# Layer 0's product in moving blocks of 512 only, multiplied and summed by VectorE, with the mean taken out beforehand

## The chip, the cores and the metric

The kernel runs on one core of a Trainium2 chip. The core has five engines with queues of their own: TensorE (PE in the profile; its weight loads are listed as PEld), VectorE (DVE), ScalarE (ACT), GpSimd (POOL) and SyncE (SP, which here only issues DMAs). Matmuls write to PSUM, from which VectorE and ScalarE read. The metric is the device time of one execution in microseconds; lower is better. Three runs of the kernel before took 760.51, 760.79 and 761.57 us.

## What is computed

A graph of N = 2048 nodes has B = 8 batches of C = 64 features. Two layers follow each other, each with a residual and a layer norm (subtract the mean over the 64 features, divide by the root of the variance):

```
w = einsum('nd,dkio->nkio', embedding, weight)     # D = 16, K = 3: a weight matrix of its own for every node
b = einsum('nd,do->no', embedding, bias)
A_stack = [I, A, 2 A A - I]
out = einsum('bnki,nkio->bno', einsum('knm,bmc->bnkc', A_stack, x), w) + b
x = layernorm(x + out)                              # layer 0
x = layernorm(x + [x, Ax, 2AAx - x, Ax, 2AAx - x] @ W1 + b1)   # layer 1
```

For layer 0 the kernel never builds `w`. For a tile of 128 nodes it computes, for each batch and each of the 16 embedding dimensions d, the product of the node features (three hops, 64 inputs each) with `weight[d]` (64 outputs), and then adds the 16 results up, each scaled with the node's own `embedding[n, d]`.

## The kernel before

The 2048 nodes are 16 tiles of 128. `z[0]`, `z[1]`, `z[2]` hold three feature arrays in SBUF, one row of 512 numbers (8 batches of 64) per node. The core goes through these stages; nearly every instruction is kept in the order in which the Python code emits it (`ordered`, `tc.keep_in_program_order`), so each engine's queue has the order of the code.

1. First hop (`hop_x`, line 526; about 7 to 123 us of the span): A times x, in 32 steps, two passes `g` over 16 row tiles.
2. Second hop (`seven_products`, line 603; 123 to 226 us): A times the first hop, split into seven block products of eight steps each. A step is eight matmuls of 512 columns. In `run` (line 266) the loads of a step are emitted four steps ahead, its operands two to four steps ahead. `more` (line 779) hangs extra work on steps: `load_weights` puts the DMAs of layer 0's weights on SP's queue, and `piece` emits one instruction of `weights()` and `weight_parts()`; they are taken from the list `todo`, two per step.
3. The mix (`mix0`, line 404, and `project`, line 475; 226 to 525 us): the product of layer 0 described above, tile after tile, with the layer norm of the tile before beside it, and layer 1's weights applied to it.
4. Two more hops for layer 1 and the final norm (`third`, `hop_g`, `hop_tile`).

The mix is where the change works. All products are made of three terms (`w_parts`: a high, a low and a mixed part of the numbers, so that float32r matmuls give full accuracy), for three hops, and two batches at once: batch 2u in partitions 0 to 63 and 2u+1 in 64 to 127. So one block of output takes 3 x 3 pairs of matmuls with 64 rows each; the two of a pair go to two PSUM banks (`pm[:, j]`). A tile's work is eight *pieces*, each filling one PSUM tile of two banks; four such tiles go round (`psum`, line 74).

- `by_batch` (line 419) makes one batch pair and eight d: 9 pairs of matmuls, 512 columns wide. ScalarE evicts it with eight scaled copies (line 430), one per d. For `g = 0` GpSimd then adds the copies up in a tree (`sum_aside`, line 444), for `g = 1` the copies are written with a stride, and VectorE sums over d with one reduce (`reduce_aside`, line 454).
- `by_four` (line 432) makes two batch pairs and four d: 18 pairs, 256 columns wide. VectorE takes it in with four scalar_tensor_tensor (line 440), each of which scales one d and adds it to the tile's sum `acc`.

A tile has four pieces of each sort, in this order; a pair (g, i) with i below 2 is `by_batch`:

```
pieces, on_vector = [(1, 0), (0, 4), (1, 1), (0, 0), (0, 1), (0, 5), (1, 4), (1, 5)], (1,)
```

The list `at[n]` holds what is emitted before piece n. `begin_sum` (line 391) starts the tile's sum with the features and the bias, in two GpSimd instructions that put the batches into the order of `acc`. `layernorm` (line 360) takes the mean with a VectorE reduce (line 363), subtracts it on GpSimd (line 366), squares on ScalarE, reduces on VectorE (line 371) and scales on GpSimd (lines 377 to 382). Beside that, `operands` (line 743) prepares the next tile: it transposes the first hop on TensorE into a PSUM tile `pt` (line 301), which ScalarE and then VectorE (lines 313 and 315) read. Late in a tile `transpose` (line 304) turns the normed tile before around, into `hT`, and `project` multiplies it with layer 1's weights into two PSUM tiles `pu`.

The last tile has another order of pieces, four that GpSimd sums and none that VectorE reduces, and among them `early` (line 860) emits the first operands of stage 4.

Of the kernel before, what the change touches and what calls it, by code (L numbers as in the profile page):

```python
# [18 lines left out]
P = 128  # L19
# [3 lines left out]
DG = 4  # L23
EPS = 1e-5
# [5 lines left out]
SPLIT = 4096.0  # L30

# [8 lines left out]
def pattern(  # L40
# [127 lines left out]

    def weights():
# [13 lines left out]
        mean = const.tile([P, 4], F32, tag="mean", name="mean")  # L183
# [15 lines left out]
    def weight_parts():  # L199
        vec = nc.vector  # L200
        yield vec.tensor_sub(w[0], w[0], w[2])
        yield vec.tensor_scalar_mul(w[2], w[2], 2.0)
        for k in (0, 2, 1):
            yield nc.scalar.copy(w_high[k], w[k])
            yield vec.tensor_tensor(w_low[k], w[k], w_high[k], ALU.subtract)
            yield vec.scalar_tensor_tensor(w[k], w_low[k], SPLIT, w_high[k], ALU.mult, ALU.add)
            yield vec.tensor_scalar_mul(w_mixed[k], w[k], SPLIT / (SPLIT - 1.0))
            yield vec.tensor_scalar_mul(w_low[k], w_low[k], -SPLIT)
        yield vec.tensor_scalar_mul(emb_sb, emb_sb, 1.0 - 1.0 / SPLIT)

# [149 lines left out]
    def layernorm(src):  # L360

        s = work.tile([P, B], F32, tag="ln_s", name="s")
        ordered(nc.vector.tensor_reduce(s, src, AX.X, ALU.add))
        ordered(nc.vector.tensor_tensor(s, s, part, ALU.mult))
        xc = xcpool.tile([P, B, C], F32, tag="ln_xc", name="xc")
        ordered(nc.gpsimd.tensor_tensor(xc, src, wide(s), ALU.subtract))
        yield xc.rearrange("p b c -> p (b c)")
        sq = squares(xc)
# [13 lines left out]
        ordered(nc.gpsimd.tensor_tensor(xc, xc, wide(r), ALU.mult))  # L382
# [7 lines left out]

    def begin_sum(t):

        acc = work.tile([P, B, C], F32, tag="acc", name="acc")
        for g in range(2):
            ordered(nc.gpsimd.tensor_tensor(
                acc[:, 4 * g : 4 * g + 4, :].rearrange("p (j i) c -> p j i c", j=2),
                bc(0, t)[:, 4 * g : 4 * g + 4, :].rearrange("p (i j) c -> p j i c", j=2),
                ebias[:, t : t + 1, :].unsqueeze(1).to_broadcast([P, 2, 2, C]), ALU.add,
            ))
        return acc  # L400
# [3 lines left out]
    def mix0(t, tt, acc, at, pieces, on_vector=()):  # L404

        def block(pm, lhsT, ds):
            for k in range(3):
                for n in range(3):
                    for j in range(2):
                        q = slice(j * C, (j + 1) * C)  # L410
                        nc.tensor.matmul(  # L411
                            pm[:, j], lhsT=tt[k][n][q, lhsT, :], rhs=w_parts[n][k][q, ds, :],
                            start=(k == 0 and n == 0), stop=(k == 2 and n == 2),
                        )

        def e(d):
            return emb_sb[:, t, d : d + 1]

        def by_batch(g, i):
            pm = bank("pm").rearrange("p j (d c) -> p j d c", c=C)  # L420
            block(pm, 2 * g + i, slice(0, 2 * DG))
            if g in on_vector:
                aside[g, i] = rawp.tile([P, 2, C, 2 * DG], F32, tag="raw", name="aside")
                to = [aside[g, i][:, :, :, d] for d in range(2 * DG)]
            else:
                if i == 0:
                    aside[g] = [rawp.tile([P, DG, 2, 2, C], F32, tag="raw", name="aside") for _ in range(2)]
                to = [aside[g][d // DG][:, d % DG, :, i, :] for d in range(2 * DG)]
            for d in range(2 * DG):
                ordered(nc.scalar.activation(to[d], pm[:, :, d, :], AF.Copy, scale=e(d)))  # L430

        def by_four(g, dg):
            dg -= 2
            pm = bank("pm").rearrange("p j (i d c) -> p j i d c", i=2, d=DG)
            for i in range(2):
                block(pm[:, :, i], 2 * g + i, slice(dg * DG, (dg + 1) * DG))
            for d in range(DG):
                part = acc[:, 4 * g : 4 * g + 4, :]
                got = pm[:, :, :, d, :].rearrange("p j i c -> p (j i) c")
                ordered(nc.vector.scalar_tensor_tensor(part, got, e(dg * DG + d), part, ALU.mult, ALU.add))  # L440

        aside = {}

        def sum_aside(g):
            one, other = [a.rearrange("p d j i c -> p d (j i) c") for a in aside[g]]
# [3 lines left out]
        def add_aside(g):  # L449
            part = acc[:, 4 * g : 4 * g + 4, :]  # L450
            one = aside[g][0][:, 0].rearrange("p j i c -> p (j i) c")
            ordered(nc.gpsimd.tensor_tensor(part, part, one, ALU.add))

        def reduce_aside(i):
            if i == 0:
                aside["sum"] = xcpool.tile([P, 2, 2, C], F32, tag="ln_xc", name="both")
            ordered(nc.vector.tensor_reduce(aside["sum"][:, i], aside[1, i], AX.X, ALU.add))

        def add_reduced(_):
            part = acc[:, 4:8, :].rearrange("p (j i) c -> p i j c", j=2)  # L460
            ordered(nc.vector.tensor_tensor(part, part, aside["sum"], ALU.add))

        does = {"sum": sum_aside, "add": add_aside, "reduce": reduce_aside, "add_reduced": add_reduced}
        for n, (g, i) in enumerate([*pieces, (None, None)]):
            for work_here in at[n]:
                if isinstance(work_here, tuple):
                    for part in work_here[0]:
                        does[part](work_here[1])
                else:
                    work_here()  # L470
            if n < len(pieces):
                (by_batch if i < 2 else by_four)(g, i)
        return layernorm(acc)
# [52 lines left out]
    def hop_x(g, kk, j):  # L526
# [45 lines left out]
        def use(got):  # L572
# [13 lines left out]
            else:  # L586
                ordered(nc.scalar.dma_start(out=corner[kk, :, g, :], in_=seen[:, 0]))
            if last and g == 1:
# [14 lines left out]
    def seven_products(s, to, sums, more, wait=4, raw=(), pairs=((0, 1), (2, 3))):  # L603
# [6 lines left out]
        def sum_of_y(kk, name):  # L610
# [11 lines left out]
            if name == "T2":  # L622
                if kk % 2 == 0:
                    tag = "acc" if kk < KK // 2 else "ln_sq"
                    kept[kk // 2] = work.tile([P, 2, BC], F32, tag=tag, name="t2")
# [109 lines left out]
    accs = []  # L735
# [40 lines left out]
    def piece():  # L776
        ordered(next(pieces))

    more = {
        (0, 3): [  # L780
# [3 lines left out]
        1: [piece] * 11,  # L784
        (2, 0): [lambda: load_weights(0, 2)],
        (3, 0): [lambda: load_weights(1)],
        2: [piece] * 8,
        3: [piece] * 8,
        4: [piece] * 2,
# [5 lines left out]
        (6, 7): [lambda: all_of(first_tile[4]), lambda: first_tile.append(begin_sum(0))],  # L795
    }
    second = seven_products(1, to_z2, sums2, more, raw=((0, 0),))
# [74 lines left out]
    acc, h, norm = first_tile[5], None, None  # L872
    tt = first_tile[0]
    coming = operands(1)
    for t in range(NT):
# [4 lines left out]
        if not last:  # L880
# [3 lines left out]
            at[1] += [n1, lambda: got.update(acc=begin_sum(t + 1))]  # L884
# [3 lines left out]
            at[2] += [n2, go(of_hop), go(of_hop), (("reduce",), 0)]  # L888
            at[3] += [root]
            at[4] += [n3, go(of_second), (("reduce",), 1), (("add_reduced",), 1)]  # L890
            if t + 2 < NT:
                at[4] += [lambda: got.update(coming=operands(t + 2))]
            at[5] += [go(of_second), go(of_second)]
            at[6] += [(("sum",), 0)]
            at[7] += [lambda: got.update(hT=transpose(h, "hT"))] if t else []
            at[7] += [(("add",), 0)]
            pieces, on_vector = [(1, 0), (0, 4), (1, 1), (0, 0), (0, 1), (0, 5), (1, 4), (1, 5)], (1,)
        else:
            at[1] += [n1, n2, root]
            at[2] += [n3, lambda: early(0, "y_high", *s)]  # L900
# [498 lines left out]
```

## Time and profile before

One execution was taken with the profiler: 761.79 us, of which the span from the first to the last instruction is 759.9 us.

| | busy, us | share of the span |
|---|---|---|
| TensorE, matmuls | 750.5 | 99% |
| VectorE | 560.4 | 74% |
| ScalarE | 455.1 | 60% |
| GpSimd | 232.9 | 31% |

The matmuls of line 411 (the pieces of the mix) carry 34% of the chain that ended last, more than any other line. TensorE's granted clock was 0.999 of full speed over the span. In the mix one tile takes 18.74 us. A busy time counts each moment once, a mean does not: the 512 evictions of line 430 have a mean of 484 ns, but with their overlap they take 143.9 us, 281 ns each. Shares over the whole span are of little use here; the views that matter are of one tile of the mix, and of the stages that get new work.

### The profile page before, as it was taken

How to read it: one execution, taken by the hardware profiler on the slowest of the kernel's cores; microseconds unless marked ns; L12 is line 12 of the kernel's file. 1: busy time of each engine (PE TensorE's matmuls, PEld its weight loads, DVE VectorE, ACT ScalarE, POOL GpSimd, SP SyncE). 2: the span in 40 equal slices, each digit the busy share in tenths (PEclk: the TensorE clock that was granted, in tenths of full speed). 3: DMA queues.
4: the chain of work that ended last, by engine and by line, in shares of the span. 5: the costliest groups of instructions: out<-in, count | busy, mean ns of one | idle time of the engine just before them, and what ended most of it. 6: DMA issues, size and time to landing. Idle time of an engine off the chain costs nothing.

```text
span 759.9 us, 15977 instructions
## 1 busy us (share of the span) xinstructions
PE 750.5 (99%) x6094; PEld 666.6 (88%) x6094; DVE 560.4 (74%) x1114; ACT 455.1 (60%) x1106; POOL 232.9 (31%) x267
## 2 busy tenths in 40 slices
PE   9999999999999999999999999999999999999996
PEld 6888888888879999999999999998788888888885
DVE  6768777678748888888888888876688548768663
ACT  5447543878756777777777777767887663112111
POOL 0000000000033666666666666656100000021431
PEclk9999999999999999999999999999999999999999
DMA  9998987555510000000000000003454454565621
GB/s 320 367 391 294 333 282 270 161 174 169 162 58 16 17 19 16 22 19 16 16 16 16 16 16 2 2 16 110 140 168 143 135 170 133 182 180 179 196 97 46
DMA packets 73700, 96.64 MB, mean 127 GB/s; under 512 B 5008, under 2 KB 48528, under 8 KB 73488
## 3 DMA queue, kind: packets, MB, share of 16 engines
q1 hardware_dynamic: 62208, 76.66, 31.9%
q10 hardware_dynamic: 11408, 18.89, 6.8%
q8 instruction: 50, 0.82, 0.5%
q14 instruction: 34, 0.28, 0.1%
HBM read 76.65 MB, written 18.87 MB: 126 GB/s over the span
## 4 chain that ended last, share of the span: by engine, by line
PE 97%; ACT 1%; POOL 1%; DMA 0%; DVE 0%; issue 0%; POOLq 0%; DVEq 0%
PE pm L411 34%; PE accT L682 27%; PE acc L255 15%; PE a L255 10%; PE accT L255 6%; PE pu L483 3%; PE pt L301 1%; PE first L143 1%; PE accT L832 1%; ACT aside L430 1%; DMA raw<-corner 0%; POOL aside L447 0%; PE accT L483 0%; PE accT L153 0%; ACT s L669 0%
## 5 line engine op out<-in xcount | busy, mean ns | idle before, releaser
L411 PE MATMUL pm<-wh,hl 64*128 64x256 f32 (+1 forms) x1152 | 214.3, 323 | 0.0
L411 PE MATMUL pm<-wm,parts 64*128 64x256 f32 (+1 forms) x1152 | 209.9, 316 | 0.0
L411 PE MATMUL pm<-wl,parts 64*128 64x256 f32 (+1 forms) x1152 | 209.7, 315 | 0.0
L682 PE MATMUL accT<-s,hl 128*128 128x512 f32 x896 | 205.7, 390 | 0.0
L682 PEld LDWEIGHTS accT<-s,hl 128*128 128x128 f32 x896 | 167.5, 188 | 35.5 <-issue 0.4
L430 ACT ACTIVATE aside<-pm,pack_sb 128x128 f32<-128x128 f32 x512 | 143.9, 484 | 20.3 <-PE pm L411 18.2
L440 DVE SCALAR_TENSOR_TENSOR acc<-pm,pack_sb,acc 128x256 f32<-128x256 f32 x256 | 123.1, 483 | 27.2 <-PE pm L411 19.7
L411 PEld LDWEIGHTS pm<-wh,hl 64*128 64x128 f32 x1152 | 135.7, 187 | 0.9 <-issue 0.5
L411 PEld LDWEIGHTS pm<-wl,parts 64*128 64x128 f32 x1152 | 135.5, 187 | 0.3
L411 PEld LDWEIGHTS pm<-wm,parts 64*128 64x128 f32 x1152 | 135.2, 186 | 0.4
L669 ACT CAST s<-raw 128x1024 fp32r<-128x1024 bf16 x104 | 109.9, 1057 | 39.5 <-ACT hl L235 28.4
L255 PE MATMUL acc<-hl,s 128*128 128x512 f32 x512 | 116.9, 390 | 0.0
L255 PEld LDWEIGHTS acc<-hl,s 128*128 128x128 f32 x512 | 96.2, 188 | 20.6 <-ACT hl L235 0.4
L447 POOL TENSOR_TENSOR aside<-aside 128x1024 f32<-128x1024 f32 (+2 forms) x51 | 75.5, 1480 | 35.5 <-ACT aside L430 32.8
L733 POOL TENSOR_TENSOR z<-z,rrow 128x512 f32<-128x512 f32 x16 | 21.1, 1319 | 212.5 <-DMA xt<-in_xT 212.5
L235 ACT CAST hl<-z 128x256 fp32r<-128x256 f32 (+1 forms) x96 | 47.8, 515 | 64.0 <-PE acc L255 24.6
L255 PE MATMUL a<-hl,s 128*128 128x512 f32 (+1 forms) x352 | 73.4, 370 | 0.0
L239 DVE TENSOR_TENSOR hl<-z,hl 128x512 fp32r<-128x512 f32 (+1 forms) x96 | 55.1, 582 | 23.1 <-ACT hl L235 13.7
L255 PEld LDWEIGHTS a<-hl,s 128*128 128x128 f32 x352 | 61.9, 188 | 11.3
L288 POOL TENSOR_TENSOR z<-z,got 128x512 f32<-128x512 f32 x3 | 4.8, 1623 | 142.6 <-ACT got L287 142.6
L492 ACT COPY z<-pu 128x256 f32<-128x256 f32 x90 | 26.3, 400 | 32.1 <-PE pu L483 32.1
L255 PE MATMUL accT<-hl,s 128*128 128x512 f32 x192 | 44.3, 390 | 0.0
(138 smaller groups left out, 848.9 us busy)
## 6 DMA issues: line engine op xcount, KB each, us to landing
raw<-in_adj SPq DMA_DIRECT2D x58, 512.0 KB, 6.4
raw<-sums_of SPq DMA_DIRECT2D x64, 256.0 KB, 2.8
sums_of<-z ACTq DMA_DIRECT2D x16, 512.0 KB, 6.8
raw<-quarters SPq DMA_DIRECT2D x32, 256.0 KB, 2.7
raw<-in_adj SPq DMA_DIRECT2D x16, 384.0 KB, 3.6
quarters<-seen ACTq DMA_DIRECT2D x16, 256.0 KB, 6.2
xt<-in_xT SPq DMA_DIRECT2D x16, 256.0 KB, 2.6
z<-in_x SPq DMA_DIRECT2D x15, 256.0 KB, 6.9
```

Source lines behind the costliest of these rows:

```text
L235: ordered(nc.scalar.copy(to[0], src))
L239: ordered(nc.vector.tensor_tensor(to[1], src, to[0], ALU.subtract))
L255: nc.tensor.matmul(accs[i], lhsT=s[:, i * P : (i + 1) * P], rhs=hl[h], start=(first and h == 0), stop=(last and h == 1),)
L411: nc.tensor.matmul(pm[:, j], lhsT=tt[k][n][q, lhsT, :], rhs=w_parts[n][k][q, ds, :], start=(k == 0 and n == 0), stop=(k == 2 and n == 2),)
L430: ordered(nc.scalar.activation(to[d], pm[:, :, d, :], AF.Copy, scale=e(d)))
L440: ordered(nc.vector.scalar_tensor_tensor(part, got, e(dg * DG + d), part, ALU.mult, ALU.add))
L447: ordered(nc.gpsimd.tensor_tensor(to, to, more, ALU.add))
L483: nc.tensor.matmul(pm[:, j, i * 3 * C : (i + 1) * 3 * C], lhsT=hT[q, 2 * g + i, :], rhs=v[q], start=True, stop=True,)
L492: ordered(nc.scalar.copy(to[k], got[:, :, :, 2 - k, :]))
L669: ordered(nc.scalar.copy(s, got["raw"]))
L682: nc.tensor.matmul(acc[i][:, c], lhsT=hl[h][:, i * P : (i + 1) * P], rhs=S[:, c * 512 : (c + 1) * 512], start=(kk == 0 and h == 0), stop=( ...
L733: ordered(nc.gpsimd.tensor_tensor(to, to, r, ALU.mult))
```

## The change

All pieces become blocks of one batch pair and eight d, 9 pairs of matmuls 512 columns wide; `by_four` is gone. A piece is (u, h, kind): batch pair u, half h of the 16 d, and who evicts it. Kind P is evicted by ScalarE and summed by GpSimd as before, kind R is evicted by ScalarE and summed by a VectorE reduce as before, and kind D is new: VectorE multiplies the whole piece with the embeddings in one tensor_tensor into an SBUF tile, and sums it with one reduce.

```diff
-        def by_four(g, dg):
-            ...
-                ordered(nc.vector.scalar_tensor_tensor(part, got, e(dg * DG + d), part, ALU.mult, ALU.add))
+        def side_by_side(a):
+            return a.rearrange("p (j c d i) -> p d j c i", j=2, i=2, d=DD)
+
+        def piece(u, h, kind):
+            ds = slice(h * DD, (h + 1) * DD)
+            pm = product(u, ds)
+            if kind == "D":
+                a = aside[u, h] = work.tile([P, 2 * C * DD], F32, tag="acc", name="aside", bufs=1)
+                e = emb_sb[:, t, ds].unsqueeze(2).to_broadcast([P, DD, 2 * C])
+                got = pm.rearrange("p j (d c i) -> p d j c i", i=2, d=DD)
+                ordered(nc.vector.tensor_tensor(side_by_side(a), got, e, ALU.mult))
+                return
+        ...
+        def reduce_aside(u, h):
+            ...
+            to = sums[h][:, 2 * u : 2 * u + 2, :].rearrange("p j (c i) -> p (j c) i", i=2)
+            src = aside[u, h].rearrange("p (c d i) -> p c i d", i=2, d=DD)
+            ordered(nc.vector.tensor_reduce(to, src, AX.X, ALU.add))
+
+        def add_reduced(h, us):
+            part = slice(2 * us[0], 2 * us[-1] + 2)
+            ordered(nc.gpsimd.tensor_tensor(acc[:, part], acc[:, part], sums[h][:, part], ALU.add))
```

In the SBUF tile of D and R, two neighbouring outputs i lie side by side and the eight d follow at a distance of two numbers, so the multiply writes pairs of numbers 64 bytes apart, and the reduce reads numbers 8 bytes apart.

The order of a tile's pieces and the work between them:

```diff
-            at[2] += [n2, go(of_hop), go(of_hop), (("reduce",), 0)]
+            at[2] += [("reduce", 0, 1), n2, go(of_hop), go(of_hop), ("reduce", 2, 0)]
-            at[4] += [n3, go(of_second), (("reduce",), 1), (("add_reduced",), 1)]
+            at[4] += [n3, go(of_second), ("reduce", 3, 0)]
-            at[5] += [go(of_second), go(of_second)]
-            at[6] += [(("sum",), 0)]
+            at[5] += [("reduce", 1, 1), go(of_second), go(of_second), ("add_reduced", 0, (2, 3))]
+            at[7] += [("reduce", 2, 1), ("sum", 0)]
-            at[7] += [(("add",), 0)]
-            pieces, on_vector = [(1, 0), (0, 4), (1, 1), (0, 0), (0, 1), (0, 5), (1, 4), (1, 5)], (1,)
+            at[8] += [("add", 0, (0, 1)), ("reduce", 3, 1), ("add_reduced", 1, everything)]
+            pieces = [(2, 0, "R"), (0, 1, "D"), (3, 0, "R"), (0, 0, "P"), (1, 1, "D"), (1, 0, "P"), (2, 1, "D"), (3, 1, "D")]
```

In the last tile the order is P, P, D, R, D, R, D, D.

The mean over the 64 outputs is taken out before: of layer 0's weights and its bias (`centre`, a VectorE reduce, a small multiply and a GpSimd subtract each) and of the features (`centre_features`, for each of the 16 tiles). A sum of centred terms has no mean, so the layer norm keeps only its scaling (`scaled_to_unit`), in place in `z[0]`:

```diff
-    def layernorm(src):
-        s = work.tile([P, B], F32, tag="ln_s", name="s")
-        ordered(nc.vector.tensor_reduce(s, src, AX.X, ALU.add))
-        ordered(nc.vector.tensor_tensor(s, s, part, ALU.mult))
-        xc = xcpool.tile([P, B, C], F32, tag="ln_xc", name="xc")
-        ordered(nc.gpsimd.tensor_tensor(xc, src, wide(s), ALU.subtract))
-        yield xc.rearrange("p b c -> p (b c)")
-        sq = squares(xc)
+    def scaled_to_unit(src):
+        sq = squares(src)
...
+    def centre_features(t):
+        s = work.tile([P, B], F32, tag="ln_s", name="s")
+        ordered(nc.vector.tensor_reduce(s, bc(0, t), AX.X, ALU.add))
+        ordered(nc.gpsimd.tensor_tensor(s, s, part, ALU.mult))
+        ordered(nc.gpsimd.tensor_tensor(bc(0, t), bc(0, t), wide(s), ALU.subtract))
     def begin_sum(t):
-        acc = work.tile([P, B, C], F32, tag="acc", name="acc")
-        for g in range(2):
-            ...
+        ordered(nc.gpsimd.tensor_tensor(bc(0, t), bc(0, t), ebias[:, t : t + 1, :].to_broadcast([P, B, C]), ALU.add))
```

`weight_parts` centres `w[0]`, `w[2]` and `w[1]`, so there are 38 pieces instead of 29, and they and the weights' DMAs start one block product earlier. Five tiles of features are centred in the first hop, eleven in the second:

```diff
-        1: [piece] * 11,
-        (2, 0): [lambda: load_weights(0, 2)],
-        (3, 0): [lambda: load_weights(1)],
+        (1, 0): [lambda: load_weights(0, 2)],
+        (2, 0): [lambda: load_weights(1)],
+        0: [piece] * 8,
+        1: [piece] * 9,
         2: [piece] * 8,
         3: [piece] * 8,
-        4: [piece] * 2,
+        4: [piece] * 5,
+        (0, 1): [lambda: [ordered(step) for step in centre(wl[:, 5:6], 4)]],
...
+    centred += [k for i in range(NT) if i % 3 == 1 for k in [i // 2 + KK * (i % 2)]]
+    left = [k for k in range(NT) if k not in centred]
+    for n, k in enumerate(left):
+        more.setdefault((1 + n // 2, 1 + n % 2 * 4), []).append(lambda k=k: centre_features(k))
```

The host hands x over with its batches reordered (0, 2, 1, 3, 4, 6, 5, 7), which spares the reordering in `begin_sum`. In the fallback `general`, which a flag selects at the end and which does not run here, one load becomes eight.

## The prediction

> **What bounds the kernel now.** First the page's busy times and the chain that ended last.
>
> ```profile
> PE 750.5 (99%) x6094; PEld 666.6 (88%) x6094; DVE 560.4 (74%) x1114; ACT 455.1 (60%) x1106; POOL 232.9 (31%) x267
> ...
> PE 97%; ACT 1%; POOL 1%; DMA 0%; DVE 0%; issue 0%; POOLq 0%; DVEq 0%
> ```
>
> TensorE carries the chain; everything else can only matter by making TensorE wait, and it waits almost nowhere. Next the busy times of one stretch of the mix, a tile long to within 0.04 us (start:end, length, then PE, PEld, DVE, ACT, POOL), and of the third block product of the second hop:
>
> ```profile
> 339.60:358.30 18.70, 18.70 (x254) 18.65 (x252) 15.21 (x29) 13.91 (x45) 12.79 (x15) 1.00 0.05 16
> ...
> 152.85:167.48 14.63, 14.63 (x66) 12.14 (x65) 10.89 (x35) 10.83 (x16) 0.00 (x0) 1.00 0.52 158
> ```
>
> In a mix tile TensorE has no gap; VectorE is the next fullest, with 3.5 us to spare. Since matmuls overlap, what a piece costs is read from starts, in TensorE's timeline:
>
> ```profile
> 339.37 0.40 PE L301 MATMUL pt<-ident,z 64*128 64x64 f32 x7
> ...
> 341.83 0.44 PE L411 MATMUL pm<-wh,hl 64*128 64x512 f32 x2
> ...
> 347.98 0.32 PE L411 MATMUL pm<-wh,hl 64*128 64x256 f32 x2
> ...
> 352.29 0.40 PE L301 MATMUL pt<-ident,xc 64*128 64x64 f32 x7
> ```
>
> From 341.83 to 347.98 run three pieces of 512, 27 pairs: 6.15 / 27 = 0.2278 us a pair. From 347.98 to 352.29 run two pieces of 256, 36 pairs: 4.31 / 36 = 0.1197 us a pair. So a piece takes 9 x 0.2278 = 2.05 us or 18 x 0.1197 = 2.155 us.
>
> Last, VectorE's timeline behind the transposes of another tile (they start at 320.63), and the last tile's stall:
>
> ```profile
> 323.34 2.05 DVE L440 SCALAR_TENSOR_TENSOR acc<-pm,pack_sb,acc 128x256 f32<-128x256 f32 x4 [0.80 <-PE pm L411]
> 325.30 0.68 DVE L371 TENSOR_REDUCE ss<-sq 128x8 f32<-128x512 f32 x1
> 325.89 0.68 DVE L315 TENSOR_TENSOR parts<-pt,hl 128x512 fp32r<-128x512 f32 x1
> ```
> ```profile
> 520.35 1.05 ACT L669 CAST s<-raw 128x1024 fp32r<-128x1024 bf16 x1 [2.65 <-DMA raw<-corner]
> ...
> 523.99 1.57 PE L483 MATMUL pu<-v,hT 64*128 64x192 f32 x16 [0.66 <-ACT hT L307]
> ```
>
> Four scaled sums take 2.05 us; then VectorE still reads `pt`, until 326.57. In the last tile ScalarE waits 2.65 us for a load, and `hT` behind it comes 0.66 us late.
>
> **The change, part by part.**
>
> *Matmuls.* In each of 16 tiles four pieces of 256 become 512: 64 x 9 x (2 x 0.1197 - 0.2278) = 6.7 us less, all of it on TensorE's path. The nearest bounds are no change in the rate per column (0) and this; I take 6.7, since blocks of both sorts run in the same tile with the same three terms, and the new pieces are the old `by_batch`.
>
> The Trainium skill puts less on it: "TensorE: Matmul & The Clock Gate", section "Back-to-back issue gap", gives a warm matmul N/2.4 ns plus 2.5 ns, so a pair merged from two would save 2.5 ns, and the sum would be an estimated 64 x 9 x 2.5 ns = 1.4 us. The row shows 11.7 ns saved, so the row is taken.
>
> *VectorE in the mix.* Per tile go 16 scaled sums at 0.483 us (7.73), the mean's reduce (0.68) and multiply (0.17), and the add of the reduced half (0.44): 9.02. Four multiplies and four reduces of 1024 come. The trace has no multiply of 1024 out of PSUM. Nearest are:
>
> ```profile
> L457 DVE TENSOR_REDUCE both<-aside 128x128 f32<-128x1024 f32 x30 | 35.6, 1190 | 0.0
> ...
> L706 DVE TENSOR_TENSOR z<-z,accT 128x512 f32<-128x512 f32 x28 | 17.9, 680 | 0.9 <-PE accT L682 0.9
> ...
> L617 DVE TENSOR_TENSOR t<-t,z 128x256 f32<-128x256 f32 x32 | 13.4, 420 | 0.5
> ...
> L205 DVE TENSOR_TENSOR wl<-w,wh 128x1024 fp32r<-128x1024 f32 x3 | 3.7, 1222 | 1.7 <-ACT wh L204 1.6
> ```
>
> 512 from PSUM take 0.680, 256 from SBUF 0.420, so 1024 come to 1.2; 1024 in SBUF take 1.222. I take 1.22 for the multiply, and 1.19 for the reduce from its own row. The far ends: 2.05, what the four scaled sums need for the same 1024 numbers, and 0.69, the one-operand instructions of 1024 (line 224). No VectorE row writes in scattered pairs; ScalarE's strided evictions take 2.31 us for eight against 2.22 for dense ones, 4%. A cheaper multiply gains nothing, as TensorE ends last. Sum: 15.2 - 9.02 + 4 x (1.22 + 1.19) = 15.8 us of a new tile of 18.74 - 4 x 0.105 = 18.32. It fits.
>
> *The tightest wait.* The fourth piece after `pt` (the fifth of the tile) takes over `pt`'s PSUM tile, and VectorE must have read it. Before, that piece starts 6.57 us after the transposes (339.37 to 345.94), and the read ends 5.94 after (320.63 to 326.57): 0.63 us to spare. After: the first piece ends at 0.27 + 2.05 = 2.32, VectorE starts 0.25 later (as 323.34 stands to the next piece's start), multiply to 3.79, reduce of it, queued directly behind, to 5.01, reduce of the squares to 5.6, `pt` read to 6.2. The piece starts at 0.27 + 3 x 2.05 = 6.42. So 0.2 us remain: hidden, and if the multiply takes 0.2 us longer every 0.1 us more costs 16 x 0.1 = 1.6 us. At 2.05 the stall is 0.63 a tile, 10 us, and the result about 3 us slower on this part.
>
> *GpSimd.* Per tile it loses the subtract (1.30) and two starts of the sum (2 x 0.754), and gets one start over 512 (1.3), an add of 256 (0.745) and one of 512 (1.3): 12.8 + 0.5 = 13.3 of 18.3. Its last add moves behind the last reduce and behind the tree, which starts one piece later; the squares on ScalarE wait for it, and behind them `pt`'s copy and the third piece's eviction. The tree starts when the sixth piece is evicted, at 0.27 + 5 x 2.05 + 0.25 + 2.3 = 13.1 after the transposes, takes 4.6, the two adds 2.05: 19.7, or 1.4 into the next tile. ScalarE is busy with the first piece's eviction until 2.6 there. 1.2 us to spare, nothing lost. ScalarE keeps its 32 evictions, 13.9 us.
>
> *The last tile.* Its period is 523.99 - 504.65 = 19.34 us from projection to projection, against 18.74 - 0.21 (no `pt`) = 18.53 undisturbed, plus about 0.25 as the projection starts cold: 1 us lost. The load waited for a buffer that GpSimd's tree frees; in the new order R pieces take one buffer each instead of two, and in the built order that load waits for the tree of the tile before. ScalarE reaches it 8.6 us into the tile (second piece done at 4.1, but squares and root until 6.05; eviction 2.2, a copy 0.4), with the data there since about 5.3 (tree and add done at 2.0, landing 3.2); then `hT` follows the sixth piece (done 12.3, evicted by 15.7) and is ready at 16.3, for a projection at 8 x 2.05 + 0.2 = 16.6. I count 0.9 us gained; the bounds are 0 and 1.1.
>
> *Before the mix.* 16 centred tiles are a reduce of 0.68 on VectorE and 0.3 + 1.3 on GpSimd, which is idle there; the weights' centring is three reduces of 1.19 and three subtracts of 2.4 (GpSimd's 1024, line 447). VectorE is fullest in the third product: its regular work 8 x 0.84 + 4 x 0.68 = 9.4, the end of `weights()` 0.75, subtract 1.22, doubling 0.68, centring 2.6, two features 1.36: 16.0 of 14.63. The cover is that a step's operands are emitted three steps, 5.5 us, ahead, so 1.4 us late in one product is caught up in the next (about 12 of 14.63). If that cover were gone, 1.4 us. SP gets the two weight loads (0.34 us issue each, 4.2 to landing) ahead of the last three loads of the second product, and the third ahead of those of the third product; the ring of six buffers is short by up to three for a product longer. A load then has three steps, 5.5 us, less the 1.06 of the copy, for a landing of 2.8: 1.6 to spare. ScalarE's copy of the third weight waits behind a GpSimd subtract; its product has 4.5 us of slack there (10.1 busy of 14.63). I cost all of this at nothing.
>
> Sum against the profiled execution: 761.79 - 6.7 - 0.9 = 754.2. That execution is 1.0 above the median of 760.79, which gives 753.2.
>
> **Rivals.**
>
> 1. *VectorE becomes the bound* (slower). Scattered writes, 64 bytes apart, make the multiply slow. It decides from 1.22 + 0.2 + 0.105 x 4 + 0.06 = 1.9 us: there the stall at `pt` eats the tile's gain and the last tile's. Doubled to 2.44, VectorE needs 15.8 + 4.9 = 20.7 a tile against 18.74 now: 16 x 2 = 31 us slower, 792. Against it speak the 4% of ScalarE's scattered writes.
> 2. *A part of the gain is lost at `pt`.* The dependent reduce or the multiply are 0.1 to 0.3 us longer than reckoned: 0 to 0.2 us a tile, up to 3 us: 753 to 757.
> 3. *The pair's price is mostly streaming:* the 512 blocks, denser now, take up to twice 0.1197: gain of the last tile alone, 759.9.
> 4. *The hop stage gets late* by VectorE's 1.4 us or a weight load of 4.2 us: 754.6 to 757.4. Against it: no wait of TensorE stands there now.
> 5. *The change does not do what it says:* excluded for the matmuls, since the built order has 576 fewer pairs; nothing moves if another engine sets the tile at 18.7: 760.8.
>
> **How the numbers follow.** Forecast (752 to 755) 0.57; rival 2 beyond that 0.08; rival 4 beyond that 0.05; rival 3 0.05, of which 0.02 within 0.2%; rival 5 0.02; rival 1 and other slow cases 0.23. 0.2% (1.5 us) is about what a measurement of this kernel can tell from no change. Faster 0.73, same 0.04, slower 0.23. The range goes from 751.5 (the whole 1.1 of the last tile and a little of third-stage start) to 764, the multiply at its upper end of 2.05 (760.8 + 3); it leaves out the deeper part of rival 1.
>
> **What would show it.** TensorE: 512 pairs at 0.228 us throughout, a tile of 18.3. VectorE: multiply near 1.22, 15.8 busy a tile. No wait of the fifth piece for VectorE. No wait of `pu` for `hT` in the last tile. Wrong it would be with multiplies above 1.9 us, or with new TensorE gaps between 123 and 226 us.

## The result and the profile after

The changed kernel takes 756.95 us (median of 5 runs, 756.62 to 757.72), the kernel before, run beside it, 760.79 (5 runs, 760.51 to 761.57): a ratio of 0.9949, 95% interval [0.9935, 0.9964]. It is faster by 3.8 us, half of the 7.6 forecast; the forecast of 753.2 is missed, and so are the 752 to 755 us that had the greatest chance; the range of 751.5 to 764.0 holds. The profiled execution after took 756.74 us with a span of 755.0, against 761.79 and 759.9 before.

The page after, busy times and the chain that ended last:

```profile
PE 744.3 (99%) x4942; PEld 613.0 (81%) x4942; DVE 618.1 (82%) x965; ACT 453.4 (60%) x1106; POOL 277.9 (37%) x299
...
PE 92%; DVE 5%; issue 1%; POOL 1%; ACT 0%; DVEq 0%; POOLq 0%
```

TensorE works 6.2 us less, but VectorE now holds 5% of the chain, where it held nothing. Two stretches of the mix after (start:end, length, then PE, PEld, DVE, ACT, POOL): from the second tile's transposes into the start of the third tile, and the same of an undisturbed tile.

```profile
244.90:263.20 18.30, 17.58 (x170) 14.46 (x168) 18.09 (x17) 13.55 (x45) 15.49 (x17) 1.00 0.06 16
338.50:356.85 18.35, 18.35 (x184) 15.35 (x182) 17.06 (x18) 13.78 (x45) 13.78 (x15) 1.00 0.06 17
```

In the undisturbed tile TensorE has no gap, as before, and VectorE works 17.06 of 18.35 us. In the earlier stretch it is full (18.09 of 18.30), and TensorE stands 0.7 us at its end. The groups that are new or have changed, after (mean ns after the busy time):

```profile
L439 DVE TENSOR_TENSOR aside<-pm,pack_sb 128x1024 f32<-128x1024 f32 x64 | 78.3, 1223 | 8.7 <-PE pm L423 6.3
L468 DVE TENSOR_REDUCE sums<-aside 128x128 f32<-128x1024 f32 x96 | 115.9, 1210 | 3.2
L332 DVE SCALAR_TENSOR_TENSOR parts<-hl,parts 128x512 fp32r<-128x512 f32 x33 | 38.7, 1173 | 1.1
```

The multiply costs 1.223 us, the reduce 1.210. The third line is a surprise: the mixed part of the next tile's operands took 0.69 us before and has a mean of 1.17 now.

Where TensorE waits, after:

```profile
PE first L145 <- DVE part L146: 1.3, 1, 1.3
PE pm L423 <- DVE aside L439: 0.7, 1, 0.7
PE accT L697 <- DVE aside L439: 0.4, 1, 0.4
PE pt L315 <- DVE aside L439: 0.3, 1, 0.3
```

Apart from the first line, which belongs to the start of the kernel, all of them are for VectorE's new multiply. A table of the stages, from the starts of TensorE's instructions (us; what changed by less than 0.2 us elsewhere is left out), says where the time went. A tile's projection comes at the end of the next tile.

| | before | after | difference | forecast |
|---|---|---|---|---|
| first hop | 116.74 | 116.89 | +0.15 | 0 |
| second hop | 103.55 | 103.69 | +0.14 | 0 |
| mix, to the first projection | 34.71 | 33.82 | -0.89 | -0.84 |
| first to second projection (third tile) | 18.74 | 19.76 | +1.02 | -0.42 |
| the next 12 tiles together | 224.88 | 220.00 | -4.88 | -5.04 |
| last tile | 19.35 | 17.97 | -1.38 | -1.32 |
| third stage, to the transposes of `hT` | 11.19 | 11.83 | +0.64 | 0 |
| last matmul to the end | 7.69 | 8.23 | +0.54 | 0 |

Everything that was forecast to shrink shrank by its amount, but for one tile. The loss is 1.44 us where the third tile begins, 0.64 at the start of the third stage, 0.54 after the last matmul and 0.14 in the second hop: 2.76 together. The first hop differs by up to 1.7 us between single executions of kernels with the same code there (116.5 to 118.2), so its +0.15 says nothing.

### The profile page after: what moved, and what is told of

It reads as the page before. It is cut to its first block, busy times and chain, and to the rows that moved or that the text cites. A ratio compares the mean times of both kernels' runs of the same rounds, so it can differ in the third digit from the quotient of the medians.

```text
span 755.0 us, 13518 instructions
## 1 busy us (share of the span) xinstructions
PE 744.3 (99%) x4942; PEld 613.0 (81%) x4942; DVE 618.1 (82%) x965; ACT 453.4 (60%) x1106; POOL 277.9 (37%) x299
## 4 chain that ended last, share of the span: by engine, by line
PE 92%; DVE 5%; issue 1%; POOL 1%; ACT 0%; DVEq 0%; POOLq 0%
PE pm L423 29%; PE accT L697 27%; PE acc L269 15%; PE a L269 10%; PE accT L269 6%; PE pu L493 2%; DVE aside L439 2%; DVE sums L468 1%; PE pt L315 1%; DVE parts L332 1%; PE first L145 1%; PE accT L853 1%; DVE parts L329 1%; ACT aside L452 0%; PE accT L493 0%
## 5 line engine op out<-in xcount | busy, mean ns | idle before, releaser
L423 PE MATMUL pm<-wh,hl 64*128 64x512 f32 x768 | 154.6, 399 | 0.7 <-DVE aside L439 0.7
L423 PE MATMUL pm<-wm,parts 64*128 64x512 f32 x768 | 150.1, 388 | 0.0
L423 PE MATMUL pm<-wl,parts 64*128 64x512 f32 x768 | 149.7, 387 | 0.0
L468 DVE TENSOR_REDUCE sums<-aside 128x128 f32<-128x1024 f32 x96 | 115.9, 1210 | 3.2
L439 DVE TENSOR_TENSOR aside<-pm,pack_sb 128x1024 f32<-128x1024 f32 x64 | 78.3, 1223 | 8.7 <-PE pm L423 6.3
L423 PEld LDWEIGHTS pm<-wm,parts 64*128 64x128 f32 x768 | 71.9, 184 | 15.7
L423 PEld LDWEIGHTS pm<-wh,hl 64*128 64x128 f32 x768 | 72.3, 185 | 15.0 <-DVE aside L439 1.0
L423 PEld LDWEIGHTS pm<-wl,parts 64*128 64x128 f32 x768 | 72.1, 185 | 13.8
L403 POOL TENSOR_TENSOR s<-s,part 128x8 f32<-128x8 f32 x16 | 7.0, 440 | 166.9 <-DVE s L402 145.8
L368 ACT ACTIVATE sq<-z 128x512 f32<-128x512 f32 x31 | 20.0, 651 | 48.8 <-DVE z L304 46.6
```

The costliest lines, as they stand in the source:

```text
L368: ordered(nc.scalar.activation(sq, src, AF.Square))
L423: nc.tensor.matmul(pm[:, j], lhsT=tt[k][n][q, u, :], rhs=w_parts[n][k][q, ds, :], start=(k == 0 and n == 0), stop=(k == 2 and n == 2),)
L439: ordered(nc.vector.tensor_tensor(side_by_side(a), got, e, ALU.mult))
L468: ordered(nc.vector.tensor_reduce(to, src, AX.X, ALU.add))
```

## Why VectorE is late: what the trace shows

VectorE at the start of the mix, after:

```profile
226.50 2.47 DVE L721 TENSOR_TENSOR z<-z,accT 128x512 f32<-128x512 f32 x4
231.56 0.70 DVE L329 TENSOR_TENSOR parts<-xt,hl 128x512 fp32r<-128x512 f32 x1 [2.59 <-ACT hl L327]
232.29 0.69 DVE L332 SCALAR_TENSOR_TENSOR parts<-hl,parts 128x512 fp32r<-128x512 f32 x1
232.90 1.22 DVE L439 TENSOR_TENSOR aside<-pm,pack_sb 128x1024 f32<-128x1024 f32 x1
```

The first multiply starts at 232.90, though its piece, the second, was done 4.8 us after the start of the mix, at 231.2. Ahead of it stand two instructions for the second tile's features, and the first of them waits for a cast that ScalarE makes only after the first piece's eight evictions. For every later tile this cast is emitted before the tile begins. The kernel before had the same order and the same times here (its first scaled sum started at 232.81); its VectorE had 3.5 us a tile to catch up, this one has 1.3. Once behind, VectorE has hardly a pause: it works 22.62 of the 23 us from 245 to 268. The second obstacle is late in the second tile, where both engines start together (all engines, after):

```profile
258.31 2.40 POOL L457 TENSOR_TENSOR aside<-aside 128x1024 f32<-128x1024 f32 x1 [0.69 <-ACT aside L452]
...
258.38 2.88 DVE L332 SCALAR_TENSOR_TENSOR parts<-hl,parts 128x512 fp32r<-128x512 f32 x1
```

An instruction of 0.69 us takes 2.88, from the start of GpSimd's add to 0.55 us past its end. This is the only tile of the trace in which it starts behind the add; in the others it starts 0.4 to 1.2 us ahead of it and takes 0.69. TensorE's waits follow at 262.45 and 265.03, in the first two pieces of the third tile. VectorE in the last tile, after:

```profile
510.13 2.35 DVE L253 TENSOR_TENSOR hl<-z,hl 128x256 fp32r<-128x256 f32 x1
...
517.49 2.35 DVE L468 TENSOR_REDUCE sums<-aside 128x128 f32<-128x1024 f32 x2
519.75 1.22 DVE L439 TENSOR_TENSOR aside<-pm,pack_sb 128x1024 f32<-128x1024 f32 x1
```

Again a low part of 0.42 us takes 2.35 beside GpSimd's tree; and the last multiply, whose piece is done at 518.0, waits behind two reduces until 519.75. The third stage wants its PSUM tile at 520.6.

**Theory:** the width of the blocks is worth the 6.7 us reckoned; about 2 us of it are lost since VectorE is late at two places, for its order and for the collisions with GpSimd. **Rivals:** VectorE is simply too full and any lateness comes up somewhere; the gain is not from the width; the centring makes the hop stages late.

## The experiments

**The changed kernel again,** in one set with the next three.

> The changed kernel once more, beside the kernels of this set, so that differences below 1 us can be read: 756.6 to 757.7 us by its first five runs. If the 1.0 us by which the first profiled execution of the kernel before lay above its median was chance, it will not be seen again; then the true gain is 3.8 us and not 5.

756.96 us (756.30 to 757.44), ratio 0.9943 [0.9929, 0.9956]; the kernel before 761.12 here, and 760.8 to 761.1 in all later sets. Its trace has the same waits: first to second projection 19.78, third stage to `hT` 11.82. The gain is 3.8 to 4.2 us, not 5: the profiled execution before lay 0.7 to 1.0 us above its medians.

**The start of the mix.**

```diff
     coming = operands(1)
+    next(coming[1])
+    next(coming[1])
...
-            at[1] += [go(of_x)] * (1 if t else 3)
+            at[1] += [go(of_x)]
```

> The conversion of the second tile's features (ScalarE's cast, VectorE's low part) is emitted ahead of the first tile, as it is for every other tile, and no more behind the first piece's eviction. Theory, VectorE starts the mix 2 us late and carries this into the second tile: VectorE's first multiply starts near 231.0 instead of 232.9, the second tile takes 18.3 to 18.6 instead of 19.73, and the kernel 1.0 to 1.4 us less, 755.5 to 756.0. Rival, VectorE is simply too full in a tile (17 to 18 us busy of 18.33) and any lateness comes up somewhere: the loss moves to another tile, 756.8 to 757.2.

755.14 us, ratio 0.9921 [0.9908, 0.9935]: 1.8 less than the changed kernel beside it, of which 1.44 by the stages. From the first to the second projection it takes 18.34 us, as in all other tiles. What TensorE waits for, and VectorE's first multiply:

```profile
PE first L145 <- DVE part L146: 1.3, 1, 1.3
PE accT L697 <- DVE aside L439: 0.4, 1, 0.4
```
```profile
230.52 1.23 DVE L439 TENSOR_TENSOR aside<-pm,pack_sb 128x1024 f32<-128x1024 f32 x1 [0.91 <-PE pm L423]
```

VectorE is now there 0.91 us before the piece is done, and both waits of the third tile are gone for good: the loss didn't move on, so VectorE is not too full. What became of the long instruction and of GpSimd's add at the end of the second tile:

```profile
257.52 0.69 DVE L332 SCALAR_TENSOR_TENSOR parts<-hl,parts 128x512 fp32r<-128x512 f32 x1
```
```profile
257.61 5.05 POOL L457 TENSOR_TENSOR aside<-aside 128x1024 f32<-128x1024 f32 x3 [0.86 <-ACT aside L452]
```

VectorE's instruction now starts 0.09 us ahead of the add instead of 0.07 behind it, and takes 0.69 us instead of 2.88. Counted from the start of the mix, the late start of 1.7 us had shrunk to 0.16 us by then in the changed kernel; the collision made it 2.35, and the waits followed. So the late start cost its 1.4 us by way of this collision; no run has the one without the other. The instructions that are stretched to 1.67 us in the later tiles are still there and cost TensorE nothing.

**The end of the mix, order.**

```diff
-            at[7] += [("reduce", 2, 1), ("reduce", 3, 0), ("add_reduced", 0, (2, 3)), ...]
-            at[8] += [("reduce", 3, 1), ...]
+            at[7] += [("reduce", 2, 1), ...]
+            at[8] += [("reduce", 3, 0), ("add_reduced", 0, (2, 3)), ("reduce", 3, 1), ...]
```

> In the last tile the reduce of the sixth piece, and the add behind it, stand after the last multiply instead of before it. Theory, the third stage's first matmuls wait for the PSUM tile of the last multiply, which waits behind two reduces: the multiply starts 1.1 us earlier, TensorE's wait of 0.41 us for it is gone, 0.4 to 0.7 us less, 756.2 to 756.6. Rival, the third stage then waits for its operands instead: no difference above 0.2 us.

756.53 us (755.32 to 757.81), ratio 0.9934 [0.9921, 0.9948]; 0.4 less by medians, which the scatter of the runs alone would not settle. The stage does: VectorE and TensorE in it,

```profile
520.18 1.22 DVE L439 TENSOR_TENSOR aside<-pm,pack_sb 128x1024 f32<-128x1024 f32 x1
521.32 2.33 DVE L468 TENSOR_REDUCE sums<-aside 128x128 f32<-128x1024 f32 x2
```
```profile
520.77 11.22 PE L697 MATMUL accT<-s,hl 128*128 128x512 f32 x48
```

the multiply ends before the third stage wants its tile, 48 matmuls run in one stretch, and from there to `hT` it is 11.15 instead of 11.82 us.

**The end of the mix, collision.**

```diff
-            at[3] += [("reduce", 0, 1), ("sum", 0), lambda: early(0, "y_low")]
+            at[3] += [("reduce", 0, 1), ("sum", 0)]
-            at[5] += [..., lambda: early(1, "y_low"), ("add", 0, (0, 1))]
+            at[5] += [..., lambda: early(0, "y_low"), lambda: early(1, "y_low"), ("add", 0, (0, 1))]
```

> In the last tile only the third stage's first low part, an instruction of VectorE with two SBUF inputs, stands two pieces later, when GpSimd's tree is over. Theory, the two engines slow each other: it takes 0.42 us instead of 2.35, GpSimd's tree somewhat less than 4.66, and the fifth piece's multiply starts 0.6 us earlier; of that 0.3 us reach the last multiply and TensorE: 756.6. Rival, the 2.35 us are the instruction's own here: it stays at 2.35 in its new place.

756.82 us, ratio 0.9946 [0.9933, 0.9960]. VectorE:

```profile
515.26 0.75 DVE L253 TENSOR_TENSOR hl<-z,hl 128x256 fp32r<-128x256 f32 x2
516.16 1.23 DVE L439 TENSOR_TENSOR aside<-pm,pack_sb 128x1024 f32<-128x1024 f32 x1
517.42 2.35 DVE L468 TENSOR_REDUCE sums<-aside 128x128 f32<-128x1024 f32 x2
519.68 1.21 DVE L439 TENSOR_TENSOR aside<-pm,pack_sb 128x1024 f32<-128x1024 f32 x1
```

Both low parts together now take 0.75 us, so the 2.35 were the collision's. But the last multiply starts only 0.07 us earlier, and the third stage to `hT` takes 11.78 us instead of 11.83. The collision is real and was not the cause here; the two reduces in front were.

**All three moves.**

> The second tile's conversion early, the sixth piece's reduce behind the last multiply, and in the last tile the first low part of the third stage two pieces later, out of the time in which GpSimd runs its tree of adds. Theory: 1.4 us of the second tile and 0.4 to 0.7 of the last come back, 754.9 to 755.6. Rival, VectorE too full: 756.5 or more.

754.70 us (754.51 to 755.49), ratio 0.9917 [0.9903, 0.9930]: 2.3 less than the changed kernel, with 18.34 from the first to the second projection and 11.15 to `hT`. The two gains add up.

**The width alone.** Each piece in two halves of 256 columns, in the same PSUM tile:

```diff
+            for half in range(2):
+                d0 = ds.start + half * (DD // 2)
+                cols = slice(half * 256, (half + 1) * 256)
...
-                            pm[:, j], ..., rhs=w_parts[n][k][q, ds, :],
+                            pm[:, j, cols], ..., rhs=w_parts[n][k][q, d0 : d0 + DD // 2, :],
```

> Every piece is made in two halves of 256 columns, 18 pairs of matmuls instead of 9, as half of the pieces were before; everything else is the changed kernel. All eight pieces are affected, so theory (a pair of 512 costs 0.2278 us, two of 256 cost 0.2394): 128 x 9 x 0.0116 = 13.4 us more on TensorE, less the 1 to 2 us that VectorE's lateness costs the changed kernel, since a tile of 19.2 us gives VectorE more room: 768 to 770. Rival, the rearrangement on VectorE and in the last tile made the gain and not the width: 757 to 759.

768.24 us, ratio 1.0105 [1.0089, 1.0120], as the theory has it. Every tile takes 19.15 us, the third one too. One of them:

```profile
318.50:337.65 19.15, 19.15 (x324) 19.15 (x324) 16.95 (x18) 13.76 (x45) 13.87 (x16) 1.00 0.05 16
```

With the same work on VectorE (16.95) a tile of all-256 blocks costs 19.15 - 18.33 = 0.82 us more, 0.1025 a piece where the rows before gave 0.105. So the width is the whole gain of an ordinary tile (the last tile gained 0.96 us beyond it), and with 0.8 us more in a tile VectorE makes up for its late start.

**The centring.** Left out: `centre` of weights and bias, `centre_features`.

```diff
-            if k in centred and g == 1:
-                centre_features(k)
```

> Left out: the subtraction of the mean from weights, bias and features ahead of the mix, and so the layer norm of layer 0 has no mean taken out. Theory, this work is hidden in the hop stages: 756.6 to 757.2. Rival, it makes the hop stages or the start of the mix late (the fourth rival of the prediction, 1.4 to 4.2 us): 755.5 or less.

755.58 us, ratio 0.9931 [0.9918, 0.9945]. By its time the rival holds, 1.4 us. By its stages it does not: the second hop takes 103.54 instead of 103.69, the mix is the same (third tile 19.75), and the time from the last matmul to the end is 7.14 instead of 8.23. There nothing is centred. The last DMAs, loads of code and the last output's store, after and without centring:

```profile
q14 instruction: 6, 0.05, 2.2%
...
out<-got SPq DMA_DIRECT2D x1, 128.0 KB, 3.2
```
```profile
q14 instruction: 5, 0.04, 1.5%
...
out<-got SPq DMA_DIRECT2D x1, 128.0 KB, 2.1
```

The store of the last output takes 3.2 us from issue to landing instead of 2.1, with one load of 8 KB of code more beside it. The two runs on this are below.

**The mean per tile.** No centring beforehand; instead a reduce and a multiply on VectorE and a subtract on GpSimd ahead of the squares:

```diff
     def scaled_to_unit(src):
+        s = work.tile([P, B], F32, tag="ln_s", name="s")
+        ordered(nc.vector.tensor_reduce(s, src, AX.X, ALU.add))
+        ordered(nc.vector.tensor_tensor(s, s, part, ALU.mult))
+        ordered(nc.gpsimd.tensor_tensor(src, src, wide(s), ALU.subtract))
```

> The mean is taken out in each tile instead of beforehand: a reduce of 512 and a small multiply on VectorE and a subtract of 512 on GpSimd ahead of the squares; the work ahead of the mix goes. VectorE then has 17.06 + 0.85 = 17.9 of 18.33 us a tile and GpSimd 13.8 + 1.3. Theory, taking the mean out beforehand is needed for the gain, since the wait at the transposes' PSUM tile has 0.1 to 0.2 us to spare and the squares come 0.5 to 1 us later: 0.4 to 1 us a tile, 763 to 772. Rival, there is room enough, and the mean's move is worth nothing by itself: 756.8 to 758.

761.37 us (11 runs), ratio 1.0006 [0.9997, 1.0015]: all of the gain is gone, though less than the 763 to 772 us of the theory. One tile:

```profile
334.60:353.20 18.60, 18.60 (x180) 15.19 (x180) 17.68 (x20) 13.58 (x45) 14.56 (x17) 1.00 0.05 15
```

A tile takes 18.60 us, 0.27 more, less than the 0.4 expected; another 2 us go in the last tile (19.92) and 1.9 on the way to `hT` (13.74 us), where TensorE waits for ScalarE's evictions and the last multiply. So the mean's move is needed: with the mean's work back in the tiles of VectorE and GpSimd, the wide blocks gain nothing.

**The collision by itself.** In the third stage, where GpSimd is idle, 24 instructions of 128 x 512 whose result is not used:

```diff
+    def beside():
+        for _ in range(3):
+            to = xcpool.tile([P, B * C], F32, tag="ln_xc", name="beside")
+            ordered(nc.gpsimd.tensor_tensor(to, z[0][0], z[0][1], ALU.add))
...
+        **{(4, kk): [beside] for kk in range(KK)},
```

> In the third stage, where GpSimd is idle, it gets 24 adds of 128 x 512 with two inputs in SBUF, whose result nobody uses (1.3 us each, some 31 us from about 575 us on). Theory, VectorE's instructions with two SBUF inputs and GpSimd's with two hinder each other: the low parts of 256 (0.42 us alone) take 0.5 to 2.3 us while GpSimd runs, the adds of the bias of 512 (0.68) 1 to 2; the instructions with one input in PSUM (0.68 and 0.475) stay within 2%. Rival, it is an effect of GpSimd's tree alone or of the mix: nothing is longer than 0.45 us.

772.72 us (two runs), ratio 1.0154 [1.0067, 1.0240]. VectorE in the changed kernel, with GpSimd idle: a low part, the add of the bias, and an add from PSUM.

```profile
576.15 0.42 DVE L253 TENSOR_TENSOR hl<-z,hl 128x256 fp32r<-128x256 f32 x1
576.49 0.42 DVE L629 TENSOR_TENSOR t<-t,z 128x256 f32<-128x256 f32 x1
576.82 0.68 DVE L506 TENSOR_TENSOR z<-z,bias 128x512 f32<-128x512 f32 x1
```

The same place beside GpSimd's adds (1.48 us each here):

```profile
578.46 1.52 DVE L253 TENSOR_TENSOR hl<-y,hl 128x256 fp32r<-128x256 f32 x1
579.90 1.50 DVE L629 TENSOR_TENSOR t<-t,z 128x256 f32<-128x256 f32 x1
581.33 1.77 DVE L506 TENSOR_TENSOR z<-z,bias 128x512 f32<-128x512 f32 x1
...
597.96 2.47 DVE L721 TENSOR_TENSOR zT<-zT,accT 128x512 f32<-128x512 f32 x4
```

Each instruction with two SBUF inputs pays about 1.1 us more, whether it has 256 or 512 numbers; four adds with one input in PSUM take 2.47 us as ever. VectorE falls behind, and the stretch from `hT` to the next hop takes 114.0 instead of 97.1 us. TensorE waits 8.9 us of the difference for VectorE. The other 8.0 go with its clock, granted at 0.91 and 0.75 in the two stretches of 25 us with the waits, which makes 8.5 us, and at 1.00 before and behind.

The same with one input, `nc.gpsimd.tensor_scalar(to, z[0][0], 1.0, 1.0, ALU.mult, ALU.add)`:

> The same 24 instructions on GpSimd, of the same size, with one SBUF input (a multiply and an add with constants). Theory, only GpSimd's second input makes the conflict: VectorE's low parts stay at 0.42 us. Rival, any stream of GpSimd in SBUF does: they are stretched as beside the adds.

759.27 us (8 runs), ratio 0.9980 [0.9968, 0.9991]; the stretch from `hT` to the next hop takes 101.1 us. The expectation falls. VectorE:

```profile
577.73 1.10 DVE L506 TENSOR_TENSOR z<-z,bias 128x512 f32<-128x512 f32 x1
578.75 0.83 DVE L253 TENSOR_TENSOR hl<-z,hl 128x256 fp32r<-128x256 f32 x1
579.50 0.83 DVE L629 TENSOR_TENSOR t<-t,z 128x256 f32<-128x256 f32 x1
```

One SBUF input of GpSimd is enough; 0.41 us is added to each, beside instructions of 0.79 us. It is VectorE's second SBUF input that matters, not GpSimd's. The Trainium skill says the same ("SBUF — State Buffer", section "Who interferes with whom"): a VectorE instruction with two SBUF inputs contends with a GpSimd instruction that reads SBUF. The runs agree on who contends; they give the sizes.

**The end of the kernel.** Two kernels with all three moves. The first has 20 more instructions on VectorE in the third stage:

```diff
+    spare = keep.tile([P, 1], F32, tag="spare", name="spare")
...
+    def filler():
+        for _ in range(5):
+            ordered(nc.vector.memset(spare, 0.0))
...
+        **{(5, kk): [filler] for kk in range(4)},
```

> The version with all three moves, with 20 more instructions on VectorE in the third stage (each sets one number per partition to zero, used by nobody), where VectorE is half idle: only the place of VectorE's later code moves. In the runs so far the time from the last matmul to the end is 8.1 to 8.6 us in every kernel with the centring beforehand and 7.1 to 7.4 without it; in the long ones VectorE's last branch comes 0.3 us later and one more load of code of 8 KB lies beside the last output's packets. Theory, it is the place of VectorE's code: 20 instructions more move it past, the branch is back to 0.3 us earlier, and the end is 0.5 to 1.1 us shorter, 753.6 to 754.2. Rival, another engine's code or the data: the end stays at 8.1 to 8.6, 754.5 to 755.0.

766.73 us, ratio 1.0075 [1.0061, 1.0089]: neither. The end itself behaves as the theory has it: 7.20 us from the last matmul instead of 8.22, one load of code less, the store landing in 2.2 us instead of 3.2. But every stage got longer, those before the new instructions too: second hop 106.52 instead of 103.67, tiles 18.52 instead of 18.34. Windows of 88 us in the second hop, of the changed kernel and of this one:

```profile
134.00:222.00 88.00, 88.00 (x390) 72.76 (x388) 82.20 (x154) 68.72 (x102) 29.91 (x30) 1.00 0.51 156
```
```profile
134.00:222.00 88.00, 88.00 (x378) 70.69 (x378) 82.46 (x159) 66.21 (x101) 26.39 (x27) 1.00 0.48 159
```

TensorE never waits, runs at full clock, and gets through 378 matmuls instead of 390. What differs in this stage is that the new `spare` tile, which takes 32 bytes per partition, lies in front of other tiles in the built program and shifts `s`, `parts` and the weights by 32 bytes, while `hl` stays. That the shift is the cause is an inference; no run had it alone.

The second moves the 16 small multiplies of `centre_features` from GpSimd to VectorE:

```diff
-        ordered(nc.gpsimd.tensor_tensor(s, s, part, ALU.mult))
+        ordered(nc.vector.tensor_tensor(s, s, part, ALU.mult))
```

> The version with all three moves, with the 16 small multiplies of the features' centring on VectorE instead of GpSimd: VectorE's code is 16 instructions longer, GpSimd's 16 shorter. If the end is short here and long with the 20 instructions on VectorE alone, GpSimd's code is the cause: then 753.6 to 754.2. If both are short, VectorE's. If both are long (754.5 to 755.0), neither, and the cause stays open. The hop stages stay within 0.2 us.

753.61 us (753.17 to 754.01), ratio 0.9901 [0.9885, 0.9916], the fastest of all: 7.2 us less than before. The second hop is the same (103.68); the end takes 7.45 us, with the last DMAs

```profile
q14 instruction: 5, 0.04, 1.4%
...
out<-got SPq DMA_DIRECT2D x1, 128.0 KB, 2.4
```

Both kernels have a short end, and what they share is that VectorE's code is longer, by 20 and by 16 instructions. Longer code on GpSimd does not do it: with 24 instructions more there, in the two runs on the collision, the end takes 8.1 and 8.4 us. Without the centring VectorE's code is shorter, and the end is short too. So the 0.5 to 1.1 us at the end go with where VectorE's code lies when the program branches past its unused part; that the place itself is the cause is inferred from these runs. The Trainium skill's "Runtime: NRT & Kernel Launch", section "Instruction fetch mechanics", says that engines load their code by DMA in blocks of 16 KiB, and that a taken branch forces a load if its target is outside the two blocks at hand. The loads are there in the trace, at the end five or six of 8 KB and one of 16 KB. Why one load more holds up the store by a microsecond stays open.

## Why the prediction was right or wrong

- *Matmuls, -6.7 us:* right. Undisturbed tiles lost 0.41 of the 0.42 us, and the halves confirm the price from the other side (0.1025 a piece). The estimate of 1.4 us by the Trainium skill's formula is ruled out by the same numbers. The section that it is from ("TensorE: Matmul & The Clock Gate", section "Back-to-back issue gap") gives the formula for one matmul by itself and says that it under- or over-counts for a stream of them.
- *VectorE's instructions, 1.22 and 1.19:* right, 1.223 and 1.210. Scattered writes cost nothing; the first rival, with multiplies above 1.9, falls.
- *VectorE's 15.8 us a tile:* wrong, 17.06. The sum took every other instruction at its old duration. Nearly 1 us is the mixed part of the features, now 1.67 us in a tile, since GpSimd's later adds lie beside it. GpSimd was reckoned at 13.3 and has 13.8. The step looked at how full each engine is and who waits for whom, and not at what two engines do to each other at the same moment.
- *The tightest wait, 0.2 us to spare at `pt`:* right in the undisturbed tiles; the read ended 6.3 us after the transposes, reckoned 6.2. The second rival's 753 to 757 us holds the measured time by chance, as its mechanism cost nothing there.
- *The tile taken as undisturbed from the first:* this is the step that failed, 1.44 us. 16 times 0.42 supposes that VectorE starts each tile on time and that its instructions keep their durations. The first tile has its own order, where the second tile's cast comes behind eight evictions. With 3.5 us of room that was harmless; with 1.3 VectorE was still 0.16 us late at the end of the second tile, and there an instruction fell behind GpSimd's add and took 2.2 us more, which reached TensorE in the third tile.
- *The last tile, -0.9 us beyond the matmuls:* right (1.38 with its matmuls, reckoned 1.32). Only the 0.25 us put on the projection's cold start was too much: from the last projection's start to the third stage the traces have 1.50 us before and 1.39 after. But the reckoning ended at the projection. Behind it the third stage needs the last multiply's PSUM tile, and two reduces were queued ahead of that multiply: 0.64 us.
- *Work before the mix, at nothing:* 0.14 us in the second hop, so the cover held. The fourth rival, whose time of 754.6 to 757.4 was met, did not happen.
- *What was in no step:* 0.54 us at the end of the kernel, up to 0.9 in the other runs, which goes with the place of VectorE's code.
- *The step to the median:* 1.0 us was taken off because the profiled execution lay that much above. The profiled execution after lay 0.2 below its own median, so the comparison of medians shows 1.2 us less than that of traces. With the 2.5 missing in the trace this adds up to the whole error of 3.75. In which stage the profiled execution before took its 1.0 us more is not known, since no other execution of that kernel was traced.

## What to carry to other kernels

When an engine's slack shrinks, cost the first and the last pass of the loop by themselves, with their own order, and follow the last one past the loop to whoever takes over its buffers: the undisturbed tile was right to 0.01 us, and two boundaries took 2.1 of the 7.6 us forecast. A lateness of 0.16 us was enough, since it changed which of two colliding instructions came first. Compare kernels stage by stage before believing a difference of a microsecond: leaving out the centring met a rival's number exactly, and most of the time came from the end of the program, where nothing had been centred. Give VectorE's instructions one input in PSUM, or another moment, where GpSimd works in SBUF.

## What was not expected of the hardware

- TensorE's clock: in the 25 us with most of the waits of 0.4 to 2.4 us, between stretches of 2 to 4 us of matmuls, the granted clock was 0.75, and 17.24 us passed for the next 64 matmuls that otherwise take 14.8. In the changed kernel, with a single wait of 0.7 us, it stayed near 1.00.
- VectorE beside GpSimd: 0.42 us becomes 1.50 beside two-input adds and 0.83 beside one-input instructions, for two SBUF inputs alone; a surcharge per instruction, not per number. Which comes first decides: 0.69 us when VectorE started 0.09 us ahead of GpSimd's add, 2.88 when it started 0.07 us behind it.
- A tile of 32 bytes put in front of others: TensorE gets through 378 instead of 390 matmuls in 88 us, without a wait; that the place of the tiles is the cause is inferred.
- The same end of the program takes 7.1 to 8.6 us, which goes with the length of VectorE's code ahead of it.
